# Moving three small pieces of a decoder's middle stages: layernorm ends, bias sums and shifted copies

## The chip, the core and the metric

The kernel runs on one core of a Trainium2 chip. The core has five engines with queues of their own: PE (TensorE, matrix products), DVE (VectorE), ACT (ScalarE), POOL (GpSimd) and SP (which only issues transfers here). Each engine works through its queue in order, and semaphores make one wait for another. The metric is the time of one launch on the device, in microseconds (us). Less is better.

## The reference, cut to what matters

The program is a decoder of four layers on 2048 tokens (32 sequences of 64, width 128, all in float32). Every sublayer ends in a layernorm of the sum with its input. The change touches two sublayers: the third of layer 0 (a local transformer of two layers) and the first of layer 1 (attention over a latent of 64).

```python
x = _layernorm(x + _L0_ffn_ref(x, L0_ffn_wqkv, ...), axis=-1)
x = _layernorm(x + _L1_attn_ref(x, L1_attn_wq, ...), axis=-1)

def _layer(x, wqkv, qs, ksc, wo, lg, lb, w1, b1, w2, b2):   # local transformer, called twice
    h = shift_token(x)              # the right half of the columns comes from the row before
    q, k, v = jnp.split(h @ wqkv, 3, axis=-1)               # 8 heads of 64
    q, k = rotary_xpos(l2norm(q) * qs, l2norm(k) * ksc)
    x = x + local_attention(q, k, v) @ wo
    h = shift_token(x)
    h = (h - mu) / jnp.sqrt(var + 1e-05) * lg + lb
    a, g = jnp.split(h @ w1 + b1, 2, axis=-1)
    return x + (a * jax.nn.gelu(g, approximate=False)) @ w2 + b2

def _layernorm(x, axis=-1, eps=1e-05):
    return (x - m) / jnp.sqrt(v + eps)
```

## The kernel before, in words

The tokens are cut into 4 blocks of 512 rows, a block into 4 tiles of 128 rows. All the work of the program is put into a table by `Steps.at(step, place, f)`. `Steps.run` calls the entries in order of step and, within a step, of place, and so fixes the order in which instructions are written. What each engine's queue then holds depends on the engine. PE is under a hand-written order in the whole program: it takes its instructions as they were written. DVE and ACT are under it only in two later stretches of steps; in the two sublayers here a scheduler picks the order of the DVE, ACT and POOL queues while the program is built. POOL and SP are never under the hand-written order.

The local transformer (`local_transformer`, lines 1083 to 1228) has 32 steps of its own, one for each tile: blocks 0 to 3 of its first layer, then blocks 0 to 3 of its second. A tile is followed through several steps by `tiles64`: `project` (products with `wqkv`, tile names `qkps` and `v`; ACT squares `sq`; DVE row sums `rn`; POOL's -0.5 power of `rn`), `twist` (DVE's three products with the rotation table into `turn`, then POOL adds the two halves and multiplies by `rn`), two steps later `turn` (PE transposes `ropeT`, ACT copies `qk`) and the scores `s`, DVE's maximum and difference, ACT's exponential `p`, and in the next step transposes `ptps`, ACT's copy `pT`, products `o`, ACT's copy `oT`, then the output product `y`, whose sum with `cur` DVE writes as `x1`. The trace names this last tile `x`.

Between blocks come pieces that belong to a whole block:

- `shifted` (lines 1094 to 1109) makes `hT`, the transposed and shifted rows of the next block. In the first layer it copies from `xT`; in the second PE first transposes `acc`, the first layer's result, into a PSUM tile `hps` (line 1103). Then ACT makes two copies of 64 partitions (lines 1105 and 1108), and POOL zeroes 8 columns (line 1107). The first `project` of the block reads `hT`.
- `normed` (line 1158) takes `x1` two blocks behind the block that begins: PE shifts it (`shps`), ACT copies it into `xs` (lines 1166 and 1167), DVE takes mean and variance `bnmv`, POOL computes `rstd` (line 440 and a power at line 346), DVE normalizes `xs` (line 1175).
- `second` (line 1203) is the last product `y<-wbig,ge`. POOL first adds the bias row to `x1` in `residual` (`resid<-x,w_rows`) and, in the second layer, the first layer's input (`resid<-resid,x`). DVE adds `resid` to the product and writes `acc`. In the second layer `norm` follows: `moments` (DVE statistics, POOL `rstd`), and `normed` of the class, in which DVE makes `nb` (line 522) and ACT writes the four tiles `x` (line 515).

The latent attention (`latent_attn`, lines 1231 to 1292) has 16 steps in the same form, with twice as many heads and its own layernorm at the end of each block. The steps of the two sublayers follow one another without a gap, so blocks 2 and 3 of the second layer end in the first steps of the latent attention.

PSUM tiles other than scores and `qkps` share four banks; `qkps` and `s` share two larger ones. Most SBUF tiles share a pool of 25 slots.

Of the kernel before, what the change touches and what calls it, by code (L numbers as in the profile page):

```python
# [17 lines left out]
ALU = mybir.AluOpType  # L18
# [263 lines left out]
class Decoder:  # L282
# [800 lines left out]
    def local_transformer(self, sp, base, names):  # L1083

        nc = self.nc
        cur, tabs = {}, []

        def tables():
            for l in range(2):
# [4 lines left out]
        hTs, x1s = {}, {}  # L1094
# [95 lines left out]
        def hidden(l, blk):  # L1190
# [9 lines left out]
                hs.append(ge)  # L1200
            ff[l, blk] = hs

        def second(l, blk):
            w, hs = self.w[names[l]], ff.pop((l, blk))
            x1 = x1s.pop((l, blk))
            xb = self.residual(x1, self.rows[f"l0f_b2{l}"])
            if l:
                self.tt(xb, xb, cur[0, blk], ALU.add, nc.gpsimd)
            y = self.ps8("G", "y2")
            for t in range(TPB):  # L1210
                for j, (o, n) in enumerate(HCH):
                    self.mm(y[:, t * P : (t + 1) * P], hs[j][:n, t * P : (t + 1) * P], w[f"w2_{j}"], j == 0, j == 2)
            x2 = self.q2([P, TPB, D], "acc")
            self.tt(x2, y.rearrange("p (t d) -> p t d", d=D), xb, ALU.add)
            if l == 0:
                cur[1, blk] = x2
            else:
                self.norm(blk, x2, pool=False)

        sp.at(base - 1, 6, tables)  # L1220
        self.tiles64(sp, base, 32, project, twist, turn, 4, lambda i: self.w[names[i // 16]]["wo"], done)
        for l in range(2):
            for blk in range(NBLK):
                n = base + 16 * l + 4 * blk
                for lag, place, f in ((-1, 7, shifted), (7, 7, normed), (8, 7, turn_h), (9, 7, hidden), (10, 3, second)):
                    sp.at(n + lag, place, lambda f=f, l=l, blk=blk: f(l, blk))
                if l:
                    sp.at(n + 12, 3, lambda blk=blk: self.turn_x(blk))


    def latent_attn(self, sp, base, name):

        nc = self.nc
        tab = self.c["r1"].rearrange("p (c s d) -> p c s d", c=2, d=64)
        lats, zs = {}, {}

        def latent(blk):
            lp = self.ps8("G", "latps")
            self.mm(lp, self.w[name]["down"], self.xT[blk])
            lats[blk] = self.q2([P, TB], "lat")  # L1240
            nc.scalar.copy(lats[blk], lp)

        def project(i):
            w = self.w[name]
            blk, t = divmod(i, TPB)
            xT, lat = self.xT[blk], lats[blk]
            tok = slice(t * P, (t + 1) * P)
            full = lambda a: a.unsqueeze(1).unsqueeze(1).to_broadcast([P, 2, 8, 64])
            qk = []
            for c in range(2):  # L1250
                ps = self.ps8("S", "qkps")
                for h in range(2):
                    o = ps[:, h * 512 : (h + 1) * 512]
                    if c == 0:
                        self.mm(o, xT[:, tok], w["wq"][:, h * 512 : (h + 1) * 512])
                    else:
                        g = slice(64 * h, 64 * h + 64)
                        self.mm(o, lat[g, tok], w["kup"][g, :])
                qk.append(self.rope64(ps, full(tab[:, c, 0, :]), full(tab[:, c, 1, :])))
            vp = [self.ps8("G", "v64").rearrange("p (n d) -> p n d", d=64) for _ in range(2)]  # L1260
            wv = w["vup"].rearrange("p (n u d) -> p n u d", u=2, d=64)
            for b in range(2):
                g = slice(64 * b, 64 * b + 64)
                for u in range(2):
                    self.mm(vp[b][64 * u : 64 * u + 64], lat[g, t * P + b * S : t * P + (b + 1) * S], wv[g, :, u, :])
            v = [self.q2([P, 8, 64], "v64") for _ in range(2)]
            for b in range(2):
                nc.scalar.copy(v[b], vp[b])
            return qk, v

        def turn(qk):
            out = []
            for c in range(2):
                d = [self.q2([P, 4, P], f"qk{c}") for _ in range(2)]
                for h in range(2):
                    self.turned64(qk[c][:, 8 * h : 8 * h + 8, :], d[h])
                out.append(d)
            return out

        def done(i, y):  # L1280
            blk, t = divmod(i, TPB)
            if t == 1:
                zs[blk] = self.q2([P, TPB, D], "z")
            r = slice(t - 1, t + 1)
            self.tt(zs[blk][:, r, :], y, self.xt[blk][:, r, :], ALU.add)
            if t == TPB - 1:
                self.norm(blk, zs.pop(blk), pool=False)

        self.tiles64(sp, base, 16, project, lambda i, t: t, turn, 8, lambda i: self.w[name]["wo"], done)
        for blk in range(NBLK):  # L1290
            sp.at(base + 4 * blk - 1, 7, lambda blk=blk: latent(blk))
            sp.at(base + 4 * blk + 9, 3, lambda blk=blk: self.turn_x(blk))


# [651 lines left out]
```

## Time and profile before

| | us |
|---|---|
| median of 3 runs | 1410.78 |
| lowest and highest run | 1400.74, 1411.97 |
| the profiled execution, launch to end | 1421.81 |
| its span in the trace | 1420.0 |
| in it: local transformer, first to last `qkps` | 149.6 to 503.3 |
| in it: latent attention, first to last `qkps` | 518.1 to 749.6 |
| PE, DVE, ACT, POOL busy between 282 and 515 us (233 us) | 203.6, 173.7, 122.0, 167.8 |

An engine's busy time is what its instructions took; an instruction's idle time before it is put down to the engine that released it. For PE the ends of instructions are modelled. The granted clock of PE over the profiled execution was 0.912 of full speed. In the timelines that follow, a row has the start in us, the duration, the engine, the line of the kernel, the operation, what it writes and reads, its shape, and in brackets the idle time before it with its releaser.

### The profile page before, as it was taken

Reading aid. Unit: us, or ns where it says so; the run is one execution under the profiler, and the core shown is the slowest. Engines: PE = TensorE matmul, PEld = TensorE weight load, DVE = VectorE, ACT = ScalarE, POOL = GpSimd, SP = SyncE. Lnnn points to the kernel's source line nnn. Section 1 sums busy time; section 2 is a strip of 40 time slices with the busy share of each in tenths; the row PEclk is TensorE's granted clock in tenths of the full one; section 3 lists DMA queues with packets and bytes.
Section 4 is the critical chain, followed back from the end, with each engine's and each line's share of the span. In section 5 each row is a group of like instructions: output and inputs, shape, how many; then the busy total and the mean of one; then the engine's idle time right before and its main releaser. Section 6 shows DMA issues by size and latency. Waiting matters only on the chain.

```text
span 1420.0 us, 37029 instructions
## 1 busy us (share of the span) xinstructions
PE 1210.3 (85%) x16009; PEld 878.6 (62%) x16009; DVE 931.3 (66%) x1856; ACT 687.8 (48%) x1172; POOL 743.0 (52%) x618
## 2 busy tenths in 40 slices
PE   7998788899888878998898998597999947889991
PEld 4775455566555555666576777594778836567771
DVE  6764667778876766765665564564668753666787
ACT  2453345555554544545454553364556524354552
POOL 3533688767876664544464244352355443335553
PEclk9999889999999989999999996697999968889995
DMA  6001010080010000010001100221001100000001
GB/s 239 3 2 26 1 46 1 21 277 2 1 55 1 1 1 1 2 68 2 2 2 35 36 4 17 73 74 33 9 2 48 37 5 25 16 9 3 2 3 30
DMA packets 33714, 43.16 MB, mean 30 GB/s; under 512 B 5946, under 2 KB 27121, under 8 KB 33168
## 3 DMA queue, kind: packets, MB, share of 16 engines
q1 hardware_dynamic: 31536, 38.20, 8.6%
q8 instruction: 126, 2.06, 0.6%
q0 software_dynamic: 2016, 2.60, 0.6%
q14 instruction: 36, 0.29, 0.1%
HBM read 26.63 MB, written 15.56 MB: 30 GB/s over the span
## 4 chain that ended last, share of the span: by engine, by line
PE 51%; DVE 20%; POOL 13%; ACT 9%; issue 5%; DMA 2%; POOLq 0%; SPq 0%; DVEq 0%; ACTq 0%
PE s L343 11%; PE o L343 9%; DVE turn L346 5%; POOL turn L346 5%; PE proj L343 5%; PE ptps L669 5%; PE qkps L343 5%; PE y L343 3%; PE ropeT L971 3%; ACT pT L671 2%; DVE p L346 2%; DVE rn L1131 2%; POOL rn L346 2%; POOL rstd L346 2%; POOL token_y L1364 2%
## 5 line engine op out<-in xcount | busy, mean ns | idle before, releaser
L346 POOL TENSOR_TENSOR turn<-turn,turn 128x1024 f32<-128x1024 f32 x64 | 150.6, 2362 | 94.1 <-DVE turn L346 93.6
L656 DVE TENSOR_REDUCE mx<-s 128x16 f32<-128x1024 f32 x96 | 117.3, 1222 | 116.3 <-PE s L343 108.7
L346 DVE TENSOR_TENSOR p<-s,mx 128x1024 f32<-128x1024 f32 (+1 forms) x144 | 159.0, 1104 | 6.0
L671 ACT COPY pT<-ptps 128x512 f32<-128x512 f32 x192 | 103.8, 588 | 83.9 <-PE ptps L669 81.9
L726 ACT ACTIVATE p<-p 128x1024 f32<-128x1024 f32 x96 | 101.4, 1056 | 53.4 <-DVE p L346 53.1
L343 PE MATMUL s<-kx,q 32*64 32x128 f32 x3072 | 110.8, 283 | 5.6 <-DVE sparts L1727 3.7
L346 DVE TENSOR_TENSOR turn<-qkps,w_const 128x512 f32<-128x512 f32 (+1 forms) x96 | 75.9, 861 | 55.6 <-PE qkps L343 55.6
L440 POOL TENSOR_SCALAR rstd<-bnmv 128x4 f32<-128x4 f32 (+1 forms) x60 | 16.7, 279 | 181.6 <-DVE bnmv L489 156.1
L343 PEld LDWEIGHTS s<-kx,q 32*64 32x64 f32 x3072 | 86.8, 136 | 37.6 <-issue 29.6
L669 PE MATMUL ptps<-w_const,p 128*128 128x128 f32 x768 | 108.5, 287 | 0.7 <-ACT p L726 0.5
L669 PEld LDWEIGHTS ptps<-w_const,p 128*128 128x128 f32 x768 | 89.6, 148 | 9.9 <-issue 8.4
L343 PEld LDWEIGHTS o<-v,pT 128*64 128x64 f32 x2176 | 74.6, 142 | 34.2 <-ACT pT L671 16.8
L594 POOL TENSOR_TENSOR kx<-k,w_const 128x1024 f32<-128x1024 f32 x31 | 60.2, 1961 | 67.2 <-ACT k L603 30.9
L346 POOL TENSOR_TENSOR rn<-rn,nhalf 128x16 f32<-128x16 f32 x32 | 93.8, 2931 | 2.7
L971 PE MATMUL ropeT<-w_const,turn 128*128 128x128 f32 x512 | 71.4, 287 | 24.6 <-ACT oT L1029 10.8
L343 PE MATMUL o<-v,pT 128*64 128x18 f32 x2176 | 83.4, 216 | 7.6 <-ACT pT L671 4.7
L971 PEld LDWEIGHTS ropeT<-w_const,turn 128*128 128x128 f32 x512 | 59.9, 147 | 36.3 <-ACT oT L1029 10.0
L346 DVE TENSOR_TENSOR turn<-qkps,xtab 128x512 f32<-128x512 f32 (+1 forms) x96 | 82.0, 858 | 0.0
L1131 DVE TENSOR_REDUCE rn<-sq 128x16 f32<-128x1024 f32 x32 | 39.0, 1218 | 62.4 <-ACT sq L1127 62.4
L509 POOL TENSOR_SCALAR x<-z,bnmv,rstd 128x128 f32<-128x128 f32 x98 | 78.1, 809 | 2.6
L343 PE MATMUL o<-pT,v 64*64 64x64 f32 x2048 | 71.8, 223 | 8.9 <-ACT pT L1013 8.9
L343 PE MATMUL qkps<-wbig,hT 128*128 128x512 f32 x128 | 71.0, 683 | 9.7 <-POOL hT L1107 8.8
(345 smaller groups left out, 2804.3 us busy)
## 6 DMA issues: line engine op xcount, KB each, us to landing
sorted_x<-zero SPq DMA_DIRECT2D x9, 990.0 KB
wbig<-in_l1f_w_dram SPq DMA_DIRECT2D x4, 1156.0 KB
wbig<-in_l2f_w_dram SPq DMA_DIRECT2D x16, 256.0 KB
wbig<-in_l0f_dram SPq DMA_DIRECT2D x2, 1561.0 KB
z<-token_y SPq DMA_DIRECT2D x8, 256.0 KB
wbig<-in_l1a_dram SPq DMA_DIRECT2D x1, 1856.0 KB
xsorted<-sorted_x SPq DMA_DIRECT2D x23, 66.0 KB
xT<-in_xT_dram SPq DMA_DIRECT2D x4, 256.0 KB
```

Source lines behind the costliest of these rows:

```text
L343: self.nc.tensor.matmul(out, lhsT=lhsT, rhs=rhs, start=start, stop=stop)
L346: (eng or self.nc.vector).tensor_tensor(out=out, in0=a, in1=b, op=op)
L440: nc.gpsimd.tensor_scalar(r[:, :n], var, EPS, None, ALU.add)
L509: eng.tensor_scalar(x[:, t0 + t, :], z[:, t0 + t, :], mv[:, t, 0:1], r[:, t : t + 1], ALU.subtract, ALU.mult)
L594: self.wide = eng.tensor_tensor(out=kx, in0=bc(kT, 1, 2), in1=bc(head[:, 2 * i : 2 * i + 2], 2, TB), op=ALU.mult).ins
L656: nc.vector.tensor_reduce(mx, s3, AX.X, ALU.max)
L669: self.nc.tensor.transpose(ps[:, j, :], flat[:, c : c + P], self.ident)
L671: self.nc.scalar.copy(o, ps)
L726: nc.scalar.activation(prs[n], prs[n], AF.Exp)
L971: self.nc.tensor.transpose(pt[:, j * P : (j + 1) * P], f[:, j * P : (j + 1) * P], self.ident)
L1131: nc.vector.tensor_reduce(rn, sq, AX.X, ALU.add)
L1364: i = self.nc.gpsimd.indirect_dma_start(dst, bass.IndirectOffsetOnAxis(at, 0), src, None, bounds_check=bound, oob_is_err=False).ins
```

## The change

Three pieces are moved in the table. No operation is added or removed, and no data is cut differently.

1. `norm` at the end of a block (second layer of the local transformer, and latent attention) is split. `moments` stays where it was; its end, `normed`, is put into the same step at place 6.6.
2. `biased`, POOL's `resid` sums, leaves `second` (step n + 10, place 3) and goes to step n + 7, place 7.1, directly behind `normed` of the same block.
3. `shifted` goes from place 7 of the step before a block, its end, to place 3.5 of that step.

```diff
+        def biased(l, blk):
+            xb = biases[blk] = self.residual(x1s[l, blk], self.rows[f"l0f_b2{l}"])
+            if l:
+                self.tt(xb, xb, cur[0, blk], ALU.add, nc.gpsimd)
+
         def second(l, blk):
             w, hs = self.w[names[l]], ff.pop((l, blk))
-            x1 = x1s.pop((l, blk))
-            xb = self.residual(x1, self.rows[f"l0f_b2{l}"])
-            if l:
-                self.tt(xb, xb, cur[0, blk], ALU.add, nc.gpsimd)
+            x1s.pop((l, blk))
+            xb = biases.pop(blk)
...
             if l == 0:
                 cur[1, blk] = x2
             else:
-                self.norm(blk, x2, pool=False)
+                ends[blk] = x2, self.moments(blk, x2)
+
+        def ended(blk):
+            x2, moments = ends.pop(blk)
+            self.normed(blk, x2, moments, False)
...
-                for lag, place, f in ((-1, 7, shifted), (7, 7, normed), (8, 7, turn_h), (9, 7, hidden), (10, 3, second)):
+                for lag, place, f in ((-1, 3.5, shifted), (7, 7, normed), (7, 7.1, biased), (8, 7, turn_h), (9, 7, hidden), (10, 3, second)):
                     sp.at(n + lag, place, lambda f=f, l=l, blk=blk: f(l, blk))
                 if l:
+                    sp.at(n + 10, 6.6, lambda blk=blk: ended(blk))
                     sp.at(n + 12, 3, lambda blk=blk: self.turn_x(blk))
...
@@ latent_attn
             if t == TPB - 1:
-                self.norm(blk, zs.pop(blk), pool=False)
+                ends[blk] = self.moments(blk, zs[blk])
+
+        def ended(blk):
+            self.normed(blk, zs.pop(blk), ends.pop(blk), False)
...
+            sp.at(base + 4 * blk + 7, 6.6, lambda blk=blk: ended(blk))
```

What the queues of the two built programs hold, compared in order, is this. The DVE and the SP queue are the same. On PE only the four transposes `hps` of each block of the second layer move: from behind `shps` to ahead of `ptps`, `y`, `o` and `shps` of the same step. On ACT, in the last step before a block:

```
before:  pT  p  oT  xs  xs  hT  hT  qk  qk
after:   hT  hT  p  pT  oT  xs  xs  qk  qk
```

(for the first block only `pT` and the two `hT` change places, for the second there is no `xs`). The ends `x` of the layernorms keep their place on ACT in all blocks but one: in the last block of the local transformer `pT  x x x x  pT  oT  oT` becomes `pT  pT  x x x  oT  x  oT`. On POOL, around the same step and three steps later:

```
before:  turn+  hT  turn*  rstd rstd   ...   rn rn  resid (resid)  turn+  turn*
after:   hT  turn+  turn*  resid (resid)  rstd rstd   ...   rn rn  turn+  turn*
```

Here `turn+` is the sum and `turn*` the product with `rn`; the second `resid` is there in the second layer only. Before blocks 2 of the first and 3 of the second layer the old place of `hT` was behind `turn*`, and before block 2 of the first layer POOL also zeroes a tile for later transfers (lines 417 and 418), formerly around `turn*`, now behind it. For the last block of all, the second `resid` stands between the two instructions of `rstd`.

More of the change, by code (lines that the diff above doesn't have):

```diff
@@ L1085, in local_transformer @@
         nc = self.nc
-        cur, tabs = {}, []
+        cur, tabs, ends, biases = {}, [], {}, {}
         def tables():
@@ L1234, in latent_attn @@
         tab = self.c["r1"].rearrange("p (c s d) -> p c s d", c=2, d=64)
-        lats, zs = {}, {}
+        lats, zs, ends = {}, {}, {}
         def latent(blk):
```

## The prediction

> **What bounds the kernel now.** I read the page's chain of waits first, to see whether one engine sets the end.
>
> ```profile
> PE 51%; DVE 20%; POOL 13%; ACT 9%; issue 5%; DMA 2%; POOLq 0%; SPq 0%; DVEq 0%; ACTq 0%
> PE s L343 11%; PE o L343 9%; DVE turn L346 5%; POOL turn L346 5%; PE proj L343 5%; PE ptps L669 5%; PE qkps L343 5%; PE y L343 3%; PE ropeT L971 3%; ACT pT L671 2%; DVE p L346 2%; DVE rn L1131 2%; POOL rn L346 2%; POOL rstd L346 2%; POOL token_y L1364 2%
> ```
>
> PE carries half of it, but no engine alone does; POOL's `turn` and `rstd` and DVE's `rn` are on it too. Only two stages are touched, so I then asked for the waits between 325 and 515 us, most of the local transformer's second layer.
>
> ```profile
> DVE xs L1175 <- POOL rstd L346: 8.6, 4, 2.3
> PE s L343 <- ACT qk L972: 8.0, 2, 4.0
> DVE acc L346 <- POOL resid L346: 6.4, 4, 2.3
> PE ropeT L971 <- ACT oT L1029: 5.7, 3, 2.2
> PE qkps L343 <- POOL hT L1107: 2.0, 1, 2.0
> ```
>
> (Total us, times, longest.) The change aims at the third and the last of these; from 190 to 325 us the last is 6.8 us in 3. Which of them move the end is told by the chain in order of time, for the step before the block at 370:
>
> ```profile
> 367.59 2.37 POOL turn L346
> 370.19 2.06 POOL turn L346
> 372.66 1.05 POOL rstd L346
> 373.73 1.12 DVE xs L1175 x4
> 374.85 1.13 DVE rn L1131
> 375.98 1.13 DVE turn L346
> 380.09 0.66 PE ropeT L971 x4
> ```
>
> The reader is to see that the chain leaves PE here: it runs through POOL's queue to `rstd`, then through DVE's, where `rn` stands behind `xs` (the squares were ready at 373.38, `rn` began at 374.76), and comes back to PE 2.2 us late at `ropeT`. The same passage stands in that chain at 234 and 326. So anything put between `turn` and `rstd` on POOL is paid in full.
>
> The other place is the end of a block in the second layer, from the timeline:
>
> ```profile
> 445.17 1.10 POOL L346 TENSOR_TENSOR resid<-x,w_rows 128x512 f32<-128x512 f32 x1
> 446.34 1.26 POOL L346 TENSOR_TENSOR resid<-resid,x 128x512 f32<-128x512 f32 x1
> 447.56 2.36 POOL L346 TENSOR_TENSOR turn<-turn,turn 128x1024 f32<-128x1024 f32 x1
> 451.99 0.55 POOL L440 TENSOR_SCALAR rstd<-bnmv 128x4 f32<-128x4 f32 x1
> 453.89 1.65 ACT L515 ACTIVATE x<-acc,nb,rstd 128x128 f32<-128x128 f32 x4 [6.10 <-DVE nb L522]
> 455.44 1.04 ACT L972 COPY qk<-ropeT 128x512 f32<-128x512 f32 x2
> 456.54 0.69 PE L343 MATMUL s<-qk,qk 64*64 64x64 f32 x32 [4.00 <-ACT qk L972]
> ```
>
> PE waits 4.0 us for `qk`, ready to copy since 449.5 but behind `x`, which waits for a `rstd` that POOL reaches only after two `resid` and two `turn`.
>
> **Part 1, ends of layernorms at 6.6: 0.** The next step's `qk` still comes after 6.6, so `x` stays ahead of it: ACT's queue is unchanged there in every block but the last (below). The stall of 4.0 us is not removed by this part.
>
> **Part 2, `resid` three steps earlier.** It issues no transfer; the SP queue is the same. Gains, where it leaves:
> - First layer, four times: DVE waited 0.93 us for it (`acc` at 268.08, 314.01, 358.10, 402.19). DVE then idles 1.82 us before the next `rn`, for squares that PE's `qkps` set. Cover: that idle time. Gain 0; if the cover were gone, 0.93 each.
> - Second layer, 445: `turn` could start when DVE's part is done, about 445.4 instead of 447.56. `rstd`, `nb`, `x`, `qk`, `s` move up by 2.1; `bnmv` would be ready at 447.9, in time. At 500.3 the same: 500.26 to 498.1, 2.15. In the latent stage at 555.7, `acc` waited 0.17 and `rstd` (557.97) then waits for `bnmv`: 0.4.
> - Last block, 617.8: `rstd` 0.6 earlier, and the second `pT` now precedes `x`. PE waited 2.14 for it (`o` at 623.84). Gain 2.1.
>
> Sum: 2.1 + 2.15 + 0.4 + 2.1 = 6.8.
>
> Costs, where it arrives, between `turn` and `rstd`. One `resid` takes 1.05 from start to start (401.07 to the `turn` at 402.12), two take 2.39 (rows above). The memset of `hT` leaves the place between the two `turn`, 0.19 (370.00 to 370.19).
> - Steps before 234.85, 326.89, 370.37: 1.05 - 0.19 = 0.86 each, 2.6.
> - Before 414.47: 2.4 - 0.2 = 2.2.
> - Before 282.48 and 467.15 `rn` waited for squares, not `xs`, because `qkps` was late behind the memset (3.05 and 1.98). At 282: `turn` ends near 281.9, zeroing 0.5, `resid` 1.05, `rstd` to `xs` 1.39, `xs` to `rn` 1.03: `rn` at 286.0 for 286.5, gain 0.5. At 467: 2.4 after 467.0, then 1.39 and 1.03: 471.8 for 471.54, loss 0.3.
> - First two steps of the latent stage: `xs` (521.10, 577.80) is followed on DVE by the `turn` that frees the PSUM tile of `s`; PE already waits for it (2.51 at 524.60, 1.53 at 581.31). Loss 2.4 each, 4.8.
>
> Sum: 2.6 + 2.2 - 0.5 + 0.3 + 4.8 = 9.4. Without slack this is exact; with slack it could be 0. In six of the eight places the follower of `xs` starts as `xs` ends, and the other two are worked out singly, so I take it whole.
>
> **Part 3, `hT` earlier.** The memset wait goes (PE: 8.8 us in 4). But ACT's new order puts `pT` behind the exponential `p`, which waits for DVE. Before 370: `p` ends at 367.57, `pT` 368.2, so `o` starts at 368.2 for 365.04; then `shps` 369.35 and `ropeT` end at 370.7: `qkps` 0.35 later, not earlier. The 1.70 that PE waited for `x` absorbs part. The other steps by the same rows: 195.01 +0.6 (`p` 190.85, `pT`, `o`, `ropeT` 1.0, `gate` 1.9: 195.6), 234.85 +1.05, 282.48 -1.6, 326.89 about 0, 467.15 -1.7. Except at 195 (no `normed`), `rn` waits for `xs`, so these are hidden or already in the sums above: 0.6 counts. Moving `hps` (0.60) fills time in which PE would wait for `pT`. Its bank is held longer; ACT copies it at once: 0. The memset waits for its slot's former readers; unseen in this trace. If the slot is still read, `turn` behind it is late: between 0 and 2.0 each, what PE waited behind the old one at 467.15, or 14 in seven steps. Below 0 it cannot go, since a wait saves nothing. I take 0, as no row of the old memset shows a wait; the other end is kept for the range. Transfers of zeros start about 2 us later: their first reader scatters at 849.6.
>
> **The clock.** PE's granted clock falls after some waits: 0.67 in 282 to 286 after 3.05 us, 0.60 in 467 to 470.4 after 1.98, but 1.00 in 380 to 384 after 2.22. A slow `qkps` takes 2.94 (282.48) against 1.88. The Trainium skill (TensorE: Matmul & The Clock Gate, Part 1) says the clock drops after an idle window of about 3.4 us, running free; the trace shows drops after less. This rule speaks against the change: the waits at 424 (2.22) and 581 (1.53) grow to 4.4 and 3.9, while those shortened, 4.0 to 1.9, have their slow phase hidden behind DVE's `x`. By the rule 2 x 1.06 = 2.1; by the trace's rows also the step at 380 (2.2 to 3.1), 3.2. I take 2.1.
>
> Total: -6.8 + 9.4 + 0.6 + 2.1 = +5.3. The profiled execution took 1421.81 (span 1420.0), 11.0 above the median 1410.78 and 9.8 above the slowest of the three. The sum would make it 1427; on the median, 1416.
>
> **Rivals.**
> - *Absorbed `rstd`* (0.17): DVE's delay is caught up before it returns to PE. Then -6.8 + 0.6: 1404.6. For it: POOL idles up to 5 us before `rn`. Against: that idle time lies behind `rstd`, and PE's 2.2 at `ropeT` follows directly.
> - *The memset pays* (0.07): PE's 8.8 us of memset waits come back whole, with 6.8: 1395. For it: 3.05 and 2.90 are large. Against: ACT's order `p`, `pT`.
> - *Slower: `pT` behind `p`* (0.19). Place: `o` in seven steps. PE's wait there grows from at most 1.7 to about 2.5, and if each is followed by a slow clock (+1.06) and a `qkps` 0.9 later, that is 7 x 2 = 14, beyond the 3.2 left without clock terms: 1428. It decides from the point where `qkps` comes about 2 us later than now, for then squares (373.4 at 370) pass `xs` (375.7 after the change). For: a 1.7 us wait at 323.8 did slow PE to 0.59. Against: three equal waits (277.85, 367.88, 411.98) did not.
> - The likeliest (0.57): `resid` moved onto the chain gives back what it gains.
>
> **Numbers.** 1416, from the likeliest. The range reaches to the absorbed case and to the slower one with the memset's upper end (1416 + 14): 1404 to 1430. A change of about 1% (14 us) is what a measurement can tell here; the three runs differ by 0.8%. Faster 0.06 (most of the memset case), slower 0.23 (0.19, and 0.04 from a likeliest case with twice the clock term), within 1% the rest, 0.71.
>
> **What would show it.** Right: waits for memset and `resid` gone; `DVE xs <- POOL rstd` up from 2.1 to 3.1 and, doubled, 4.4; PE's `s <- ACT qk` at 2 instead of 4; latent `s` waiting 4 to 5; ACT `x` in place. Wrong: `rn` directly at its squares after `xs`, or `qkps` starting 2 us later than the steps above say.

## The result, and the profile after

| | us |
|---|---|
| before, median of 20 runs (lowest to highest) | 1407.27 (1400.53 to 1413.7) |
| changed, median of 20 runs (lowest to highest) | 1416.2 (1406.66 to 1421.92) |
| ratio, 95% interval | 1.0065 [1.0051, 1.0080], +9.2 us [+7.2, +11.3] |
| profiled execution of the changed kernel, and its span | 1414.35, 1412.5 |

The time was predicted at 1416, within 1% of before, and it is. The effect behind it was predicted at +5.3 us and is +9.2: before came out 3.5 us lower in the larger set of runs than in the three that the prediction had. So the forecast holds, but that 1416.2 meets 1416 so closely is luck: a sum that was 3.9 us too small stands on a start that was 3.5 us too high. The sections below look for what the sum left out.

The changed kernel's profiled span is 7.5 us *shorter* than the one of before. That says nothing of the change: from the router to the end (835 us in the profile before, 845 after) the program is the same, and that stretch took 584.5 us before and 567.5 after. In the other profiles of this study it took 580.7 to 591.0. What the change did is read ahead of that point, where the changed kernel is 12.4 us longer (the first `sq` of the local transformer at 153.39 before and 150.42 after, the router's first maximum at 835.52 and 844.98).

The waits between 325 and 517 us, the changed kernel (total us, times, longest):

```profile
DVE xs L1175 <- POOL rstd L346: 12.8, 4, 4.5
PE o L343 <- ACT pT L1013: 10.9, 8, 2.8
PE ropeT L971 <- ACT oT L1029: 10.3, 4, 4.5
PE s L343 <- ACT qk L972: 6.6, 2, 3.3
```

No wait for the memset or for `resid` is left in this window. `xs` waits 12.8 us for `rstd` instead of 8.6, and PE at `ropeT` 10.3 instead of 5.7. PE's new wait at `o` for `pT` is the price of ACT's order `p`, `pT`.

The chain in order of time for the step before the block at 375, the answer to the chain at 367.59 before:

```profile
370.24 2.36 POOL turn L346
372.60 0.07 issue
372.67 2.23 POOL turn L346
374.89 1.05 POOL resid L346
375.95 0.08 issue
376.03 0.24 POOL rstd L440
...
376.35 1.05 POOL rstd L346
377.39 0.03 issue
377.42 1.11 DVE xs L1175 x4
378.53 1.13 DVE rn L1131
```

`resid` stands in the chain with its full 1.05 us, between POOL's `turn` and `rstd`, and nothing absorbs it.

The end of a block in the second layer, from the changed kernel's timeline, beside the rows at 445 to 456 before:

```profile
453.83 0.68 DVE L346 TENSOR_TENSOR acc<-y,resid 128x512 f32<-128x512 f32 x1
453.99 2.35 POOL L346 TENSOR_TENSOR turn<-turn,turn 128x1024 f32<-128x1024 f32 x1 [0.25 <-DVE turn L346]
...
459.13 1.04 POOL L346 TENSOR_TENSOR rstd<-rstd,nhalf 128x4 f32<-128x4 f32 x1
460.20 0.16 DVE L522 SCALAR_TENSOR_TENSOR nb<-bnmv,rstd 128x4 f32<-128x4 f32 x1 [3.23 <-POOL rstd L346]
460.39 1.65 ACT L515 ACTIVATE x<-acc,nb,rstd 128x128 f32<-128x128 f32 x4 [4.11 <-DVE nb L522]
461.95 1.04 ACT L972 COPY qk<-ropeT 128x512 f32<-128x512 f32 x2
463.04 0.75 PE L343 MATMUL s<-qk,qk 64*64 64x64 f32 x32 [3.31 <-ACT qk L972]
```

POOL's `turn` starts as soon as DVE's part is done, and this step is 2.04 us shorter than before (the one at 509, 2.05). `x` is still ahead of `qk`, and PE still waits for it.

What the chain does not show is the clock. These are PE's rows behind the block at 420 us, in the timeline of the changed kernel:

```profile
426.79 0.60 PE L971 MATMUL ropeT<-w_const,turn 128*128 128x128 f32 x4
430.44 1.11 PE L971 MATMUL ropeT<-w_const,turn 128*128 128x128 f32 x4 [3.06 <-ACT oT L1029]
431.35 3.62 PE L343 MATMUL qkps<-wbig,hT 128*128 128x512 f32 x4
```

and the same place before:

```profile
424.19 0.66 PE L971 MATMUL ropeT<-w_const,turn 128*128 128x128 f32 x4 [2.22 <-ACT oT L1029]
424.68 1.88 PE L343 MATMUL qkps<-wbig,hT 128*128 128x512 f32 x4
```

Behind a wait of 3.06 us the four `qkps` take 3.62 us, behind 2.22 they took 1.88. The granted clock in the windows of these `qkps` is 0.50 after and 1.00 before. PE's wait itself is not the loss: ACT copies `oT` only behind the exponential `p`, which waits for DVE, so PE could not go on sooner. The loss is what comes after it.

The clock also falls in the step before, behind PE's new wait for `pT`. The changed kernel:

```profile
416.07 1.97 PE L343 MATMUL o<-pT,v 64*64 64x64 f32 x32 [2.75 <-ACT pT L1013]
417.98 1.22 PE L343 MATMUL shps<-x,w_const 128*128 128x256 f32 x2
418.99 1.14 PE L971 MATMUL ropeT<-w_const,turn 128*128 128x128 f32 x8
```

and before:

```profile
409.13 1.15 PE L343 MATMUL o<-pT,v 64*64 64x64 f32 x32
411.98 0.70 PE L343 MATMUL shps<-x,w_const 128*128 128x256 f32 x2 [1.70 <-DVE x L346]
412.95 1.04 PE L971 MATMUL ropeT<-w_const,turn 128*128 128x128 f32 x8
```

The granted clock is 0.59 in the first of these stretches. Whether that delay reaches DVE is told in the section on the prediction.

### The profile page after: what moved, and what is told of

The parts are those of the page before. It is cut to its first block, busy times and chain, and to the rows that moved or that the text cites. A ratio compares the mean times of both kernels' runs of the same rounds, so it can differ in the third digit from the quotient of the medians.

```text
span 1412.5 us, 37033 instructions
## 1 busy us (share of the span) xinstructions
PE 1200.6 (85%) x16009; PEld 871.1 (62%) x16009; DVE 929.0 (66%) x1856; ACT 686.8 (49%) x1172; POOL 743.4 (53%) x618
## 3 DMA queue, kind: packets, MB, share of 16 engines
q8 instruction: 126, 2.06, 0.6%
## 4 chain that ended last, share of the span: by engine, by line
PE 51%; DVE 22%; POOL 10%; ACT 9%; issue 5%; DMA 2%; POOLq 0%; SPq 0%; DVEq 0%; ACTq 0%
PE s L343 10%; PE o L343 9%; DVE turn L346 7%; PE qkps L343 5%; PE proj L343 5%; PE ptps L669 4%; POOL turn L346 4%; PE y L343 3%; PE ropeT L971 3%; DVE p L346 2%; ACT pT L671 2%; DVE rn L1131 2%; POOL rstd L346 2%; POOL token_y L1376 2%; DVE mx L990 1%
## 5 line engine op out<-in xcount | busy, mean ns | idle before, releaser
L669 PE MATMUL ptps<-w_const,p 128*128 128x128 f32 x768 | 105.6, 281 | 0.7 <-ACT p L726 0.5
L343 PE MATMUL o<-v,pT 128*64 128x18 f32 x2176 | 80.4, 214 | 5.4 <-ACT pT L671 4.2
L343 PEld LDWEIGHTS o<-pT,v 64*64 64x64 f32 x2048 | 65.4, 138 | 30.2 <-ACT pT L1013 26.2
```

The costliest lines, as they stand in the source:

```text
L343: self.nc.tensor.matmul(out, lhsT=lhsT, rhs=rhs, start=start, stop=stop)
L669: self.nc.tensor.transpose(ps[:, j, :], flat[:, c : c + P], self.ident)
```

## The experiments

All ratios are against the kernel before, run on the same chip beside each group; the groups ran on different chips. "Moved" is the ratio less 1, times the median of before. "Touched stages" is one profiled execution of each, from the first `sq` of the local transformer to the router's first maximum; before it is 682.1 us, changed 694.6. Two executions of one program (the copies alone) differ by 7.1 us in it.

| run | ratio, 95% interval | moved, us | touched stages, us |
|---|---|---|---|
| copies alone, at 3.5 | 1.0035 [1.0018, 1.0052] | +5.0 [+2.6, +7.4] | 679.8 |
| the same again | 1.0006 [0.9987, 1.0026] | +0.9 [-1.8, +3.7] | 686.9 |
| copies alone, at 4.5 | 1.0017 [1.0000, 1.0034] | +2.4 [0.0, +4.8] | 685.5 |
| sums alone | 1.0061 [1.0038, 1.0083] | +8.7 [+5.4, +11.8] | 691.5 |
| ends alone | 0.9963 [0.9948, 0.9978] | -5.3 [-7.4, -3.1] | 678.7 |
| all three, sums behind `rstd` | 1.0038 [1.0021, 1.0055] | +5.4 [+3.0, +7.8] | 684.7 |
| all three, sums in the gap | 0.9950 [0.9929, 0.9971] | -7.1 [-10.1, -4.1] | 673.0 |
| ends, and sums in the gap | 0.9902 [0.9865, 0.9938] | -13.9 [-19.2, -8.8] | 668.9 |
| the same, `x` behind `qk` | 0.9907 [0.9877, 0.9936] | -13.2 [-17.5, -9.1] | 667.6 |
| ends, sums in the gap, copies at 4.5 | 0.9946 [0.9924, 0.9968] | -7.7 [-10.8, -4.6] | 677.7 |
| the same, PE's wait filled | 0.9888 [0.9871, 0.9905] | -15.9 [-18.3, -13.5] | 669.8 |
| changed, PE's wait filled | 1.0056 [1.0034, 1.0077] | +8.0 [+4.8, +10.9] | 688.9 |

### The three parts, each alone

```diff
-                for lag, place, f in ((-1, 7, shifted), (7, 7, normed), (8, 7, turn_h), (9, 7, hidden), (10, 3, second)):
+                for lag, place, f in ((-1, 3.5, shifted), (7, 7, normed), (8, 7, turn_h), (9, 7, hidden), (10, 3, second)):
```

> The kernel before with part 3 alone (copies of the next block's rows at place 3.5). Theory A (the sum as it stands, corrected by the trace after: what costs is resid between turn and rstd on POOL, and a slower TensorE clock behind the longer wait it makes): the memset is about neutral on POOL's chain, qkps comes up to 2 us earlier where it was late, so -2 us against before, between -4 and +1, with xs <- POOL rstd still at 2.1 to 2.3. Rival B (pT behind p delays o, and the wait of o slows the clock): +7 to +12 us, nearly all of what the whole change costs. PE o <- ACT pT should stand near 11 us in the window of the second layer by both.

+5.0 us, between the two theories and outside both ranges. The sums alone (`biased` at step n + 7, place 7.1; `ended` directly behind its statistics):

> The kernel before with part 2 alone (resid three steps earlier, between turn and rstd; layernorm ends directly behind their statistics). Theory A: the arrivals cost 1.05 three times, 2.4 at 414, 0.4 at 467, and 4.8 in the latent stage, 6 to 8 us with what the clock adds; the departures give back 4.2 to 6.8: +5 to +10 us against before, about the whole of the change. Rival B: only the departures show, -2 to -7 us. Absorbed rstd: -5 to -7 us.

+8.7 us: theory A. At 331, 379 and 427 us in its profile DVE's `rn` falls back by a further 1.05, 1.04 and 2.36 us against before, one, one and two `resid`. Rival B and the absorbed `rstd` both wanted a gain, and fall as explanations of this part. The ends alone (part 1, with `resid` just ahead of `second`):

> The kernel before with part 1 alone (ends of layernorms at place 6.6). All queues stay as before but ACT's in the last block of the local transformer, where the second pT now precedes x. Prediction: 0 elsewhere, and up to -2.1 us there (PE's wait of 2.14 us for that pT): -1 to -2 us by both theories. A third reading, that the place of the ends changes more than this: outside of -4 to +2.

-5.3 us, outside the -4 to +2 that the expectation set as the mark of a third reading (the ends change more than this), though its interval reaches in. By its queues that reading has no ground: DVE, ACT and POOL hold the same order as before but for the `pT` and `oT` of the last block. The step of the last block is 3.05 us shorter, and its rows say why. Before:

```profile
623.84 1.29 PE L343 MATMUL o<-pT,v 64*64 64x64 f32 x32 [2.14 <-ACT pT L1013]
625.06 3.43 PE L971 MATMUL ropeT<-w_const,turn 128*128 128x128 f32 x16
```

The wait of 2.14 us is gone with `pT` ahead of `x`; so is what it left behind, 16 `ropeT` in 3.43 us (16 take 1.91 in the changed kernel's profile, at 619.61). The touched stages of this profile are 3.4 us shorter, which lies within the interval of the time; whether the other 2 us are there at all is open.

### The sums behind `rstd` instead of ahead of it

```diff
-(7, 7.1, biased)
+(8, 1.5, biased)
```

> The changed kernel with resid put at step n + 8, place 1.5, so that POOL takes it directly behind rstd instead of ahead of it; DVE, ACT, PE and SP queues are those of the changed kernel. Theory A: the departures' gain of 6 to 7 us stays, the cost on rstd goes and with it the slow clock behind it: -8 us against before (-4 to -12), xs <- POOL rstd back at 2.1 to 2.3 us each. Rival B: the time of the changed kernel less 1 to 2 us, +5 to +8 us against before.

+5.4 us, where -8 was expected: this expectation failed. `rstd` does come back to its time, but the timeline of this run shows what happens next:

```profile
424.83 1.04 POOL L346 TENSOR_TENSOR rstd<-rstd,nhalf 128x4 f32<-128x4 f32 x1
425.84 1.09 POOL L346 TENSOR_TENSOR resid<-x,w_rows 128x512 f32<-128x512 f32 x1
425.90 2.98 DVE L1175 TENSOR_SCALAR xs<-xs,bnmv,rstd 128x128 f32<-128x128 f32 x4 [1.94 <-POOL rstd L346]
427.01 1.27 POOL L346 TENSOR_TENSOR resid<-resid,x 128x512 f32<-128x512 f32 x1
428.81 1.20 DVE L1131 TENSOR_REDUCE rn<-sq 128x16 f32<-128x1024 f32 x1
```

DVE's four `xs` take 2.98 us beside two `resid` and 1.88 beside one (at 240, 288, 334 and 381); they take 1.11 or 1.12 before, in the changed kernel and in the gap run below. The durations of one `xs` in this run are 0.33 to 1.43 us (median 0.34), in the changed kernel 0.34 to 0.35. The Trainium skill (SBUF — State Buffer, "SBUF: two separate sides") says that VectorE and GpSimd share one pair of ports as an exclusive lock, and that an operation of VectorE in a two-port mode stands still while GpSimd holds it. The rows agree with the lock: four `xs` are 0.8 and 1.9 us longer beside 1.09 and 2.36 us of `resid`. One by one it is plainer still: the first `xs` ends at 427.01 and the second at 428.37, each 0.08 us behind the end of a `resid` (426.93 and 428.29), and the other two take 0.33. In which mode `xs` ran, no row shows. So the delay did not go, it changed from POOL's queue to DVE. Rival B's number, +5 to +8, fits the time but not these rows.

### The sums where neither engine needs them away

Between POOL's `turn` and its `rn` of a middle step POOL idles, and DVE runs `rn` and `turn` from PSUM. There `resid` can stand (`shifted` back at place 7, part 1 as changed):

```diff
-((-1, 3.5, shifted), (7, 7, normed), (7, 7.1, biased), (8, 7, turn_h), (9, 7, hidden), (10, 3, second))
+((-1, 7, shifted), (7, 7, normed), (9, 1.5, biased), (8, 7, turn_h), (9, 7, hidden), (10, 3, second))
```

> Parts 1 and 2 with the copies where they were before, and resid at step n + 9, place 1.5: POOL takes it between turn and rn of a middle step, where POOL idled 1.8 us and more for squares and DVE ran nothing. Theory (resid costs only where DVE or rstd waits for POOL, be it in POOL's queue or because DVE's xs stands still while resid runs, as in the run behind rstd): the departures' 2.05 twice and the 5.2 of part 1 alone, -8 to -11 us against before, with xs <- POOL rstd at 2.1 to 2.3 and xs of 0.34 us each. If a sum three steps ahead costs wherever it is put: -5 us at most, +3 at worst.

-13.9 us, beyond the -8 to -11 expected. The `xs` are back at 1.12 each, with waits of 2.10 to 2.32 (but for 4.87 at the first block):

```profile
325.97 1.11 DVE L1175 TENSOR_SCALAR xs<-xs,bnmv,rstd 128x128 f32<-128x128 f32 x4 [2.11 <-POOL rstd L346]
414.14 1.12 DVE L1175 TENSOR_SCALAR xs<-xs,bnmv,rstd 128x128 f32<-128x128 f32 x4 [2.11 <-POOL rstd L346]
```

The same single edit in the changed kernel, with its copies at 3.5:

> The changed kernel with one edit: resid goes to step n + 9, place 1.5, into POOL's gap between turn and rn of a middle step; parts 1 and 3 stay as changed, and the PE, ACT, DVE and SP queues are those of the changed kernel. If the change's cost is resid's arrival on the chain to rstd, and the clock behind the longer wait: the gap run's -13.9 us and the 0 to 5 us of the copies alone, -8 to -13 us against before, 17 to 22 us faster than the changed kernel, with xs <- POOL rstd at 2.1 to 2.3. If pT behind p were the larger part (the rival): at most the 5 to 6 us of the departures back, +3 us or more.

-7.1 us, just short of the -8 to -13 expected. Against the changed kernel's +9.2 that is 16 us for the place of 12 POOL instructions (21.6 us in the touched stages of the two profiles; the DVE and ACT queues hold the same order). The rival, at best +3, falls as the larger part. The two kernels with the sums in the gap differ in the early copies alone; their intervals overlap and they ran on two chips, and the profiles differ by 4.1 us. Then `x` behind `qk` (`ended` of the local transformer at step n + 11, place 0.5):

> The run of both parts with resid in the gap, and the layernorm ends of the local transformer moved to step n + 11, place 0.5, so that ACT copies qk ahead of the four x. PE's wait s <- ACT qk (8.0 us in 2 before, about 4 in 2 with resid gone) should vanish. If that wait is on the path: 3 to 4 us faster than the run with the gap alone, -11 to -15 us against before; if DVE's turn and p, not s, set the step there: the same as that run.

-13.2 us, the same as without. PE's wait for `qk` is gone and the time is not, within an interval of 4 us to either side. In single profiles the two steps are 0.96 us shorter each; the times can't tell that.

### What the early copies cost

At place 4.5 the copies come early too, but ACT has `pT` ahead of `p` again:

> The kernel before with part 3 alone, but at place 4.5 instead of 3.5: ACT keeps pT ahead of the first copy and of the exponential p (order pT, hT, p, hT, oT), and POOL's memset stands ahead of turn as in the run of part 3 alone. That run was 5.0 us slower than before by the medians. If pT behind p is what costs there, this one is not slower: 0 to -5 us against before, and PE o <- ACT pT falls from 22.5 us to about 5. If the memset's place on POOL, or the earlier copies themselves, cost it: +3 to +5 us again.

+2.4 us. `o <- pT` falls from 22.5 to 5.9 us (190 to 517 us) as expected, but the kernel is no faster than before. So `pT` behind `p` is not all of it. Together with the gap:

> The run before this one with the copies at place 4.5 as well. If the waits for the memset (8.8 us in 4 on PE) are worth something once pT is ahead of p: 1 to 4 us faster than that run, -9 to -14 us against before. If qkps a little earlier is hidden behind rstd and xs: the same as that run. If copies cost by their own: up to 5 us slower than that run.

-7.7 us, 6 us slower than the gap alone on the same chip (the two intervals overlap by 2 us; the touched stages of the profiles differ by 8.8). The windows of its `qkps` behind five blocks (window, its length, busy PE, PEld, DVE, ACT, POOL with counts, granted clock, DMA share, GB/s) give a reason:

```profile
245.90:249.00 3.10, 3.10 (x6) 1.03 (x4) 1.50 (x1) 0.80 (x2) 3.02 (x2) 0.50 0.00 0
292.20:295.00 2.80, 2.80 (x6) 1.08 (x4) 1.55 (x1) 0.85 (x2) 2.72 (x2) 0.56 1.06 367
338.00:341.00 3.00, 3.00 (x6) 1.13 (x4) 1.52 (x1) 0.90 (x2) 2.92 (x2) 0.50 0.00 0
384.40:387.40 3.00, 3.00 (x6) 1.03 (x4) 1.50 (x1) 0.80 (x2) 2.92 (x2) 0.59 0.00 0
430.10:433.00 2.90, 2.90 (x6) 1.09 (x4) 1.56 (x1) 0.86 (x2) 2.82 (x2) 0.50 0.00 0
```

Half the clock in all five, behind waits at `ropeT` of 4.42, 3.48, 3.51, 3.43 and 3.42 us. In the gap run the waits there are 2.2 to 2.3 in the three from 332 on, and `qkps` takes 1.88. With early copies PE loses no time at the memset, does its `qkps` 1.1 us earlier, and then waits at `ropeT` that much longer for an `oT` that is no earlier: two short waits have become one long one, behind which the clock is down. To see whether that costs the time, PE was given more work inside this wait, and nothing was taken away:

```diff
         pt = self.ps8("G", "ropeT")
         f = t.rearrange("p h d -> p (h d)")
+        for _ in range(self.again):
+            for j in range(4):
+                self.nc.tensor.transpose(pt[:, j * P : (j + 1) * P], f[:, j * P : (j + 1) * P], self.ident)
+        self.again = 0
...
         def rotate(i):
             t, v = st[i]
+            self.again = 4 if nh == 4 and i in (7, 11, 15, 19, 23) else 0
```

> The run with resid in the gap and the copies at place 4.5, with the first four ropeT transposes made five times in the steps behind five blocks, where PE waited 3.4 to 4.4 us and the qkps behind took 3.08 to 3.62 us instead of 1.88. Clock theory: qkps at 1.9 in all five, 5 to 8 us faster than that run (-7.7 us against before): -12 to -16 us, level with the gap alone (-13.9) or a little better. If copies that come earlier cost in another way: -5 to -9 us as that run.

-15.9 us, 8 us faster for 80 more transposes. With the gap alone (-13.9) and with `x` behind `qk` (-13.2) it is among the fastest kernels here; these can't be told apart. The windows of the same five `qkps`:

```profile
245.50:247.50 2.00, 2.00 (x8) 0.76 (x8) 1.91 (x1) 1.18 (x4) 1.92 (x2) 1.00 0.00 0
289.70:291.50 1.80, 1.80 (x6) 0.58 (x4) 1.80 (x1) 1.10 (x3) 1.72 (x2) 1.00 1.06 360
333.80:335.80 2.00, 2.00 (x8) 0.76 (x8) 1.92 (x1) 1.18 (x4) 1.92 (x2) 1.00 0.00 0
378.00:380.00 2.00, 2.00 (x8) 0.76 (x8) 1.89 (x1) 1.18 (x4) 1.92 (x2) 1.00 0.00 0
422.10:424.10 2.00, 2.00 (x8) 0.76 (x8) 1.93 (x1) 1.17 (x4) 1.92 (x2) 1.00 0.03 8
```

Its interval and that of the run without the filling do not touch, though the two ran on different chips. The five `qkps` took 17.0 us together without the filling and take 9.4 with it, and the touched stages are 7.9 us shorter. This shows the clock as a cost of its own. In the changed kernel itself, filled in three places (tiles 7, 23 and 27):

> The changed kernel with more work for PE and none less: in the steps behind the blocks at 234, 424 and 480 us PE makes the first four ropeT transposes five times instead of once (48 transposes of 0.15 us more in all, 7 us, into the same tile), inside the waits of 4.42, 3.06 and 4.48 us that stand ahead of the second ropeT. If those waits cost by the TensorE clock that falls behind them (qkps 3.62, 3.62 and 3.33 us there, 1.88 behind waits of 1.3 and 1.4): qkps back at 1.9 to 2.0 in the three, and 3 to 6 us faster than the changed kernel, +3 to +6 us against before. If the clock is not the cause, or its fall is hidden: +9 us against before as the changed kernel, or more by the added work.

+8.0 us [+4.8, +10.9], not to be told from the changed kernel's +9.2 [+7.2, +11.3]: by its time this run decides nothing. By its profile the touched stages are 5.6 us shorter than the changed kernel's, `qkps` takes 1.88 in two of the three places (433 and 484 us), and the six steps from the block at 420 us on are together 4.0 us shorter than in the changed kernel's profile; in the third the wait did not come about in that execution, and another `qkps`, at 238.67, was slow instead.

Last, the copies alone once more:

> The kernel before with part 3 alone (copies at place 3.5), once more, for a second profiled execution: the first one was 12 us faster than the median of its own runs and showed granted clocks of 1.00 behind the blocks at 320, 370, 415 and 470 us. If the clock is what the typical run loses: this profile shows PE waits of 2.7 us or more at o followed by qkps of 3 us and more in two or more of these places, and a time near +5 us against before. If not: the same touched stages as in the first profile, and the difference lies behind 830 us, where nothing was changed.

+0.9 us this time. Of the four places, only two have a slow `qkps`, of 2.78 and 2.40 us, where two of 3 us or more and a time near +5 were expected: this expectation failed. Two others are slow further up (3.62 at 243.61, 2.98 at 290.47) where the first profile has 1.88. The two executions of this one program differ by 3.8 us between the first and the last `sq` of the local transformer. What the copies alone cost is thus between nothing and 5 us, and the clock's part in it differs from one execution to the next.

## Why the prediction was right, and where its sum was not

Term by term, in us. The measured column is the difference of the two profiles, from one landmark to the next (squares `sq`, DVE's `rn`, maxima).

| term of the sum | predicted | measured |
|---|---|---|
| `resid` arriving, six steps, up to `rn` | +4.6 | +6.1 |
| behind these `rn`, up to the next squares: the clock | +1.06 | +6.2 |
| first steps of the latent stage, with clock and the 0.4 at 555.7 | +5.5 | +6.3 |
| step at 195 | +0.6 | +0.1 |
| step ahead of it, 172 to 186, where nothing has moved yet | 0 | +1.1 |
| `resid` leaving, 445 and 500 | -4.25 | -4.1 |
| last block | -2.1 | -3.5 |
| sum | +5.4 | +12.2 |

- *Part 1: 0 but for the last block.* The ACT order is as said, the gain of the last block is there, and it belongs to this part and not to the sums, where the prediction booked it. Its size was 2.1 and is 3.5 (3.05 in the run of part 1 alone), because the slow clock behind the wait goes with it.
- *Part 2, departures.* 2.04 and 2.05 for 2.1 and 2.15: the rows carried it. The wait of `s` for `qk` was to fall to 2 and fell to 3.31, since PE's own work ahead of it came earlier too: the step's length is what counts, not the wait.
- *Part 2, arrivals.* The mechanism is shown, by the chain, by the sums alone (+8.7), and by taking them away (16 us). One `resid` was put at 0.86 and costs 1.17 in the steps before 329 and 375. The memset's 0.19 was credited for leaving its place between the two `turn`, but it brought nothing: the second `turn` takes 2.23 us where it took 2.06 right behind the memset. Why, no row shows. At 282 the gain of 0.5 came out as 0.1, at 467 the loss of 0.3 as 0.4.
- *Absorbed `rstd`* fell (sums alone). *The memset pays* fell: its waits went, and the copies alone brought nothing back.
- *Part 3 and the slower rival.* `pT` behind `p` is there as described: PE waits 2.75 to 3.65 us at `o` in six of the seven steps. And the clock does fall behind these waits, as the rival said: in five of the six the granted clock from `o` to `qkps` is 0.58 to 0.70, and the work from `o` to the end of `qkps` takes 1.4 to 1.8 us longer than at the full clock of the sixth (229), though `qkps` itself is back near 1.88 in all but one (2.52 at 329.15). In the changed kernel this is hidden, as the prediction had it: the squares are still ready before `xs` ends (at 375: 377.85 and 378.53), since `resid` makes `xs` late. Without `resid` on the chain it is not: in the copies alone (first profile, against before) and in the changed kernel with its sums in the gap (against the gap run), `rn` follows its squares and falls back by 0.5 to 0.6 us in each of the three steps around 330, 370 and 420. So the rival named a real cost, but one that the changed kernel covers. With `pT` ahead of `p` (copies at 4.5) the clock is lost at `ropeT` instead.
- *The clock: the term that was mis-sized.* The prediction took 1.06 us each for two waits at `ropeT` and `s`, at 424 and 581. Both lost the clock, but so did three more: at 234 the wait at `ropeT` grew from 2.39 to 4.42, at 282 from 0.20 to 2.09, and at 480 it is new, 4.48. From `rn` to the next squares the steps behind 234, 282, 424 and 480 are 0.96, 1.30, 2.22 and 1.74 us longer than before, 6.2 together for the one 1.06 that the sum had there; `qkps` alone went from 3.07, 1.88, 1.88 and 1.88 to 3.62, 3.19, 3.62 and 3.33.
- *Why these waits grew.* Two delays that the sum had kept apart meet at one wait: `resid` makes `oT` later, and at 282 and 480 PE arrives earlier, without the wait for the memset (its squares move up by 1.3 and 3.8 us). The prediction booked an earlier `qkps` as hidden, at 0; it is hidden only from DVE. At 234 PE was early by luck: the `qkps` at 223 had been slow before (3.01) and was not now (1.88). Where PE comes later, by its waits at `o`, it goes the other way: at 380 the wait that was to grow to 3.1 shrank to 1.44, and at 424 it grew to 3.06 instead of 4.4.

In the prediction a rule of an idle window of about 3.4 us was weighed (the Trainium skill, TensorE: Matmul & The Clock Gate, Part 1). Applied to every wait that grows it would have named 234 and 480 as well, but neither 282 nor 424 with the waits that were measured. Over all profiles of this study, every wait of 3.4 us or more at `ropeT` in the steps behind a block was followed by a `qkps` of 2.78 to 3.62 us, sixteen in all. Waits of 2.20 to 2.27 behind the blocks at 320 to 425 us were followed by 1.88, eleven in all (before, ends alone, gap, `x` behind `qk`). From 2.38 to 3.30 it went either way: 2.39 was followed by 3.07 (before, 244.77), 2.61 by 2.98, 3.06 by 3.62, but 2.40 and 2.71 by 1.88. And three shorter waits, of 1.97, 2.09 and 2.12 us, were followed by 3.27, 3.19 and 3.52. So a wait of the rule's length did cost the clock at `ropeT` every time, but a wait of 2 us could cost it too, which the page's length does not cover: by these runs the length of the wait alone does not decide.

Right among the signs: no memset or `resid` waits, ACT's `x` in place, latent `s` waiting 4.90 and 3.68. The wait of `xs` (2.3 to 4.5) is a poor sign, since the early `bnmv` lets DVE start waiting sooner.

The profiles differ by 12.4 us in the touched stages, the medians by 9.2 [7.2, 11.3]. One pair of executions is no measure of a term that differs from one execution to the next as the clock's does. The step at 172 to 186 shows it: the wait there is 2.28 us in both profiles and nothing around it has moved, but eight `ropeT` behind it take 1.97 us in the changed kernel's execution and 1.15 in that of before. Not shown are the other 2 us of part 1, what the clock alone costs in the changed kernel's typical run, and why short waits cost the clock in one place and not in another.

## What to carry to other kernels

Moving work off one wait is worth only what the engine at the end of the chain gets; ask of each new place whether a dependent instruction stands behind it in the same queue, and which operation of a neighbour engine it stops while it runs. A step that comes earlier while the one that it feeds does not only makes the next wait longer, and on PE a longer wait can cost more than the one removed. Where such a wait can't be shortened, repeating work inside it can pay (8 us here for 80 transposes, which brought the kernel back level with the one that had no early copies).

## What the runs showed of the hardware

- POOL's `resid` (128x512, float32, 1.1 to 1.3 us) and DVE's `xs` (128x128, float32, one tensor and two scalars) do not run side by side: one `xs` takes up to 1.43 us instead of 0.34. DVE's `rn` and its `turn` from PSUM keep their 1.22 and 0.68 beside the same `resid` (gap run, 424 to 427 us).
- The granted clock can be down behind a PE wait and back before the next large product: behind 2.75 us at `o` (changed kernel, 416 us) it was 0.59 up to 419.9, the 32 `o` took 1.97 us instead of 1.15, and `qkps` right behind took its 1.88. Looking at `qkps` alone misses it.
- Executions of one unchanged stretch of this program, from the router to the end, took 567.5 to 591.0 us over the profiles; the span that was 7.5 us shorter was that of the slower kernel.
